# A state-space layer and an outlook layer on one core: a norm chain planned a chunk earlier, a bias that becomes a row of weights, and a product that changes its place in the step

## The chip, the cores and the metric

The kernel runs on one core of one Trainium2 chip. The metric is device time in microseconds (us) of one execution; the kernel before was run three times, and the profile is of one execution more. All data is 32-bit floating point.

The core's engines work from queues of their own, each strictly in the order of its queue, and meet only in semaphores: PE multiplies matrices, ACT applies functions and copies, DVE and POOL do elementwise work, SP issues the transfers. In the code they are `pe`, `ae`, `ve`, `gp` and `sp`. The wrapper `InOrder` (line 40 is its issue, which is why nearly every row of the profile says L40) keeps each engine's instructions in the order in which the program issues them. What an instruction stands behind in its queue is thus read from the program.

## What is computed

There are two layers, each with a residual; the input is 4 images of 384 channels by 4096 positions. The change is in the first.

```python
x = x + L0(group_norm(x))
# L0, per image, positions l in order:
xn = layer_norm(xs) * ln_w + ln_b
xb, z = split(xn @ in_proj_w.T)                 # 768 channels each
xc = silu(causal_conv4(xb) + conv_b)
dt_r, Bm, Cm = split(xc @ x_proj_w.T)           # 24 + 16 + 16
dt = softplus(dt_r @ dt_w.T + dt_b)             # 768 channels
h  = exp(dt * A) * h + (dt * xc) * B            # 768 x 16 states, a recurrence over l
y  = sum_n(h * C) + xc * D
out = (y * silu(z)) @ out_proj_w.T
x = x + L1(group_norm(x))                       # outlook attention, not touched
```

## The kernel before: chunks, units, steps and slots

The first layer (`mamba_layer`) cuts each image's 4096 positions into chunks of 241 (the last of an image has 240), 17 per image, 68 in all. The recurrence of a chunk is cut into 12 **units** (`NU`) of 64 of the 768 channels. One loop runs over **steps** `s`; step `s` runs the recurrence of unit `s`, so a chunk takes 12 steps. In this text a step is named by `m`, its number within the chunk in hand, 0 to 11.

In each step the main loop issues, in this order: the fetch of inputs for unit s+4 (even steps, on SP, eight transfers), the slot EARLY, `s_inputs2` (DVE, half of the product dt*x*B of unit s+1), `s_gate` (DVE, on even steps, for unit s-3), the slot READY, then twice a recurrence `s_scan` on DVE and the decays `s_decay` on ACT (four exponentials of one half of unit s+1), with `s_carry` (ACT) after the first half and `s_save` (DVE, copies the last states away) after the second recurrence. Then come `s_outputs` (POOL, h times C of unit s-1), the slot POOL, `s_inputs` (POOL, the other half of dt*x*B of unit s+2), `s_sum` of unit s-2 (PE; on odd steps ahead of the slot MID, on even steps behind it), MID and LATE.

Everything else, that is, the projections and norms that make a later chunk's inputs (the **front**) and the output projection of a finished chunk (the **end**), is put into these slots by hand. The dictionary `plan` gives, for a step counted from two chunks ahead of the chunk's own start, and for a slot, what is issued; `ends` does so for the end. `parts` looks both up and issues what is due.

The pieces of the front, with the engine of each: `f_load` (SP); the norm chain `f_mean` (PE), `f_center` (DVE, writes `u`), `f_square` (ACT, writes `sq`), `f_var` (PE, `ps_var`), `f_root` (DVE, `vs`), `f_pow` (POOL), `f_rs` (PE, `ps_rs`), `f_scale` (DVE, `u` again); the projections `f_x(0..2)` and `f_z(0..2)` (PE 12 matmul instructions each, copied out by ACT to `xb` and `zs`); `f_conv(0..2)` (PE 16 each, ACT to `xc`); `f_gates` (ACT, Silu of `xc` and `zs` in place, a table load ahead of it and one behind); `f_bc` (PE, `ps_xd`), `f_xd` (ACT copies to `xd`, SP stores it); `f_dt(0..2)` (PE, `ps_dt`), `f_softplus` (ACT, to `dt`; in its wake, in `f_dts`, SP fetches B and C into `bc` in eight transfers and stores `dt` for later fetches), `f_dtx` (DVE, dt*xc, stored by SP for later fetches); `f_b` (PE, replicates B into `bp`). The end is `e_load`, `e_project(0..2)` (PE `ps_out`, ACT copies to `xr`) and `e_store` (DVE statistics, SP).

Buffers that couple the engines: all of the front's and end's PSUM results share a ring of two tiles (`pmm`, tag `mm`); the sums `y` have a single tile, so the first sum of a pair of units waits for `s_gate` of the pair before; the decays have two tiles `da`, one per half; `h` has five; fetched inputs have three.

Where the change bears, the plan before puts, in steps m of the chunk in hand: `f_mean` and `f_center` at the very end of step 2, `f_var` in 5, `f_root` and `f_dt(1)` at the start of 6, then, in the same step 6, the six softplus with `f_dt(2)` among them, `f_rs` at the start of 7, and `f_scale` and `f_dtx` ahead of the recurrences of 7. The projections go from 8 to 1, the gates into LATE of 2, `f_bc` into 4. The end's three projections are in 3, 6 and 8.

Of the kernel before, what the change touches and what calls it, by code (L numbers as in the profile page):

```python
# [5 lines left out]
F32 = mybir.dt.float32  # L6
AF = mybir.ActivationFunctionType
# [3 lines left out]
P = 128  # L11
C = 384
NCB = C // P
DI = 768
NJ = DI // P
NS = 16
RK = 24
KC = 4
TM = 241
CG = 32  # L20
# [64 lines left out]
def mamba_layer(ctx, tc, x, w, x1, sc1, bi1, consts):  # L85
# [78 lines left out]
    def norm_part():  # L164

        if norms:
            try:
                next(norms[0])
            except StopIteration:
                norms.pop(0)  # L170
# [13 lines left out]
    cw = load("cw", [P, NJ, KC])  # L184
    cbias = load("cbias", [P, NJ])
    wx = load("wx", [P, NJ, 2 * NS + RK])
    wdt = wp.tile([2 * NS + RK, DI], F32, tag="wdt", name="wdt")
    sp.dma_start(wdt[2 * NS :, :], w["wdt"])
    dtb = load("dtb", [P, NJ])
    ssum = load("ssum", [P, CG])  # L190
    alog = load("alog", [P, NQ, NG])
    dvec = load("dvec", [P, NJ])
# [10 lines left out]
    sel = wp.tile([2 * NS, NG // 2, P], F32, tag="sel", name="sel")  # L203
    sp.dma_start(sel, w["sel"])
    pw = pmm.tile([P, 2, TM], F32, tag="mm", name="pw")
    for j in range(2 * NJ):
        for cb in range(NCB):
# [4 lines left out]
                start=(cb == 0),  # L212
                stop=(cb == NCB - 1),
# [16 lines left out]
    chunks = [(b, ci, t0, min(TM, L - t0)) for b in range(B) for ci, t0 in enumerate(range(0, L, TM))]  # L230
    NC = -(-L // TM)
    NU = NQ // 2
# [5 lines left out]
    live = {}  # L238
# [15 lines left out]
    def f_center(c):  # L254

        t = c.t
        c.u = front.tile([P, NCB, TM], F32, tag="u", name="u")
        ve.scalar_tensor_tensor(
            c.u[:, :, :t],
            c.xt[:, :, :t],  # L260
            c.sc,
            c.ps[:, 0:1, :t].to_broadcast([P, NCB, t]),
            ALU.mult,
            ALU.subtract,
        )
# [117 lines left out]
    def f_xd(c):  # L383

        t, px = c.t, c.px
        c.xd = front.tile([2 * NS + RK, TM], F32, tag="xd", name="xd")
        ae.copy(c.xd[:, :t], px[: 2 * NS + RK, 0, :t])
        bcd = dram.tile([2, NG, 4, TM], F32, tag="bcd", name="bcd")
        sp.dma_start(bcd[:, :, :, :t].rearrange("k g r t -> (k g r) t"), c.xd[: 2 * NS, :t])
        c.bcd = bcd  # L390

    def f_dt(c, jj):
        t = c.t
        if jj == 0:
            c.dt = front.tile([P, NJ, TM], F32, tag="dt", name="dt")
            c.pdt = {}
        pp = pmm.tile([P, 2, TM], F32, tag="mm", name="ps_dt")
        for h in range(2):
            j = 2 * jj + h
            pe.matmul(  # L400
                pp[:, h, :t], wdt[2 * NS :, j * P : (j + 1) * P], c.xd[2 * NS :, :t], start=True, stop=True
            )
        c.pdt[jj] = pp

    def f_softplus(c, jj):
        t = c.t
        for h in range(2):
            j = 2 * jj + h
            ae.activation(c.dt[:, j, :t], c.pdt[jj][:, h, :t], AF.Softplus, bias=dtb[:, j : j + 1])

    def f_dts(c):
        t = c.t
        f_softplus(c, 0)
        f_dt(c, 2)
        f_softplus(c, 1)
        f_softplus(c, 2)
        c.bc = []
        for k in range(2):
            m = cross.tile([P, NG, TM], F32, tag=f"bc{k}", name=f"bc{k}")
            for r in range(4):  # L420
                sp.dma_start(
                    m[CG * r : CG * (r + 1), :, :t], c.bcd[k, :, r, :t].unsqueeze(0).to_broadcast([CG, NG, t])
                )
            c.bc.append(m)
        c.dtd = dram.tile([NJ, P, TM], F32, tag="dtd", name="dtd")
        sp.dma_start(c.dtd[:, :, :t].rearrange("j p t -> p j t"), c.dt[:, :, :t])

    def f_b(c):

        for g in range(ND):  # L430
            pe.matmul(bp[:, g, : c.t], sel[:, g, :], c.xd[: 2 * NS, : c.t], start=True, stop=True)

    def f_dtx(c):
        t = c.t
# [5 lines left out]

    EARLY, READY, POOL, MID, LATE = range(5)

    def at(f, *args):
        return lambda c: f(c, *args)

    plan = {
        (0, MID): [f_load],
        (2, LATE): [f_mean, f_center],  # L450
        (3, LATE): [f_square],
        (5, MID): [f_var],
        (6, EARLY): [f_root],
        (6, POOL): [f_pow],
        (7, EARLY): [f_rs],
        (7, READY): [f_scale],
        (8, MID): [at(f_x, 0)],
        (9, MID): [at(f_x, 1), at(f_z, 0)],
        (10, LATE): [at(f_x, 2)],
        (11, MID): [at(f_conv, 0), at(f_z, 1)],  # L460
        (12, MID): [at(f_conv, 1)],
        (13, MID): [at(f_conv, 2), at(f_z, 2)],
        (14, LATE): [f_gates],
        (16, MID): [f_bc],
        (16, LATE): [f_xd],
        (17, LATE): [at(f_dt, 0)],
        (18, EARLY): [at(f_dt, 1)],
        (18, READY): [f_dts],
        (19, READY): [f_dtx],
        (22, MID): [f_b],  # L470
    }

# [8 lines left out]
    bp = pbb.tile([P, 2, TM], F32, tag="bp", name="bp")  # L481
# [16 lines left out]
    def unit(n):  # L498
        if not 0 <= n < NU * len(chunks):
            return None  # L500
        if n not in units:
            units[n] = Unit(n)
        return units[n]
# [86 lines left out]
    def s_gate(u):  # L590
        c, t = u.c, u.t
        ve.tensor_mul(c.zs[:, u.j, :t], u.y[:, :t], c.zs[:, u.j, :t])
# [18 lines left out]
    def e_store(c):  # L611
# [12 lines left out]
                )  # L624
            )


    ends = {
        (-3, MID): [e_load],
        (3, MID): [at(e_project, 0)],  # L630
        (6, LATE): [at(e_project, 1)],
        (8, LATE): [at(e_project, 2)],
        (10, READY): [e_store],
    }

    def parts(s, when):

        for k in (s // NU + 3, s // NU + 2, s // NU + 1):
            if 0 <= k < len(chunks):
                for part in plan.get((s - NU * (k - 2), when), []):  # L640
                    if k not in live:
                        c = live[k] = Chunk()
                        c.b, c.ci, c.t0, c.t = chunks[k]
                    part(live[k])
        for k in (s // NU, s // NU - 1):
            if 0 <= k < len(chunks):
                for part in ends.get((s - NU * (k + 1), when), []):
                    part(live[k])

    pending = {}  # L650
    for s in range(-2 * NU, NU * (len(chunks) + 2)):
        k, m = divmod(s, NU)
        if m % 2 == 0 and unit(s + 4) is not None:
            s_fetch(s + 4)
        parts(s, EARLY)
        norm_part()

        if (u := unit(s + 1)) is not None:
            s_inputs2(u)
        if (u := unit(s - 3)) is not None and not u.first:  # L660
            s_gate(u)
        parts(s, READY)

        b, ci = chunks[k][:2] if 0 <= k < len(chunks) else (B, 0)
        if b + 1 < B:
            i, e = divmod(m - 2, 6)
            if ci < NX // 2 and e == 0:
                pending[i] = x_load(b + 1, 2 * ci + i)
            if ci < NX // 2 and e == 2:
                x_stat(b + 1, 2 * ci + i, pending[i])  # L670
            if ci == NX // 2 and m == 6:
                x_coeffs(b + 1)
        for i in range(2):
            if (u := unit(s)) is not None:
                s_scan(u, i)
                if i == 1:
                    s_save(u)
            if (u := unit(s + 1)) is not None:
                s_decay(u, i)
                if i == 0:  # L680
                    s_carry(u)
        if (u := unit(s - 1)) is not None:
            s_outputs(u)
        parts(s, POOL)
        if (u := unit(s + 2)) is not None:
            s_inputs(u)

# [320 lines left out]
def layouts(inputs):  # L1008
# [3 lines left out]
    g = {k: np.asarray(v) for k, v in inputs.items()}  # L1012
    c = np.ascontiguousarray

    def inner(v):
        v = v.reshape(NJ, P, *v.shape[1:])
        return c(np.swapaxes(v, 0, 1))

    a = {}
# [5 lines left out]
    a["cbias"] = inner(g["L0_conv_conv_b"])  # L1025
    wx = g["L0_conv_x_proj_w"]
    a["wx"] = inner(np.concatenate([wx[RK:], wx[:RK]], 0).T)
    a["wdt"] = c(g["L0_conv_dt_w"].T)
    a["dtb"] = inner(g["L0_conv_dt_b"])
    a["alog"] = c(  # L1030
        g["L0_conv_A_log"].reshape(NQ, CG, NG, 4).transpose(3, 1, 0, 2).reshape(P, NQ, NG)
    )
# [16 lines left out]
    r = np.arange(P)  # L1049
    k = np.arange(2 * NS)  # L1050
# [22 lines left out]
```

## Time and profile before

| | |
|---|---|
| three runs | 7261.19, 7263.74 (median), 7266.12 us |
| profiled execution: its own time | 7263.01 us |
| profiled execution: span | 7261.2 us, clock granted to PE 0.895 of full |
| busy share of the span | PE 88%, DVE 78%, POOL 75%, ACT 68% |
| first layer's steady stretch, 120 to 5860 us | PE 5033.63, DVE 4892.31, POOL 4833.87, ACT 4251.41 us busy of 5740; clock 0.88 |
| second layer, 5985 to 7261 us | PE 1226.91 us busy of 1276; clock 0.98 |
| one period of the steady stretch | `dtx` at 2591.16 and again at 2676.49 us: 85.33 us for a chunk of 12 steps |

A page of the profile lists, for each group of instructions, its busy time, the mean of one, and the idle time of the engine ahead of it with what ended it. The timeline gives instructions of one engine in order of time: start, duration of the run of them, names, count, and in brackets the idle time before and what ended it. A wait "<-PE ps_rs" was ended by PE's writing of `ps_rs`. The chain of work is followed back from the last instruction, at each step to what released it. Idle time of an engine that nobody waits for costs nothing.

### The profile page before, as it was taken

Reading aid. Unit: us, or ns where it says so; the run is one execution under the profiler, and the core shown is the slowest. Engines: PE = TensorE matmul, PEld = TensorE weight load, DVE = VectorE, ACT = ScalarE, POOL = GpSimd, SP = SyncE. Lnnn points to the kernel's source line nnn. Section 1 sums busy time; section 2 is a strip of 40 time slices with the busy share of each in tenths; the row PEclk is TensorE's granted clock in tenths of the full one; section 3 lists DMA queues with packets and bytes.
Section 4 is the critical chain, followed back from the end, with each engine's and each line's share of the span. In section 5 each row is a group of like instructions: output and inputs, shape, how many; then the busy total and the mean of one; then the engine's idle time right before and its main releaser. Section 6 shows DMA issues by size and latency. Waiting matters only on the chain.

```text
span 7261.2 us, 112696 instructions
## 1 busy us (share of the span) xinstructions
PE 6411.3 (88%) x40440; PEld 4301.2 (59%) x40440; DVE 5628.1 (78%) x5688; ACT 4933.4 (68%) x10865; POOL 5426.0 (75%) x2101
## 2 busy tenths in 40 slices
PE   6888888888888888888888888888888868999999
PEld 5666566565565666655656666655656634555555
DVE  4888888888888888888888888888888874444444
ACT  3777777777777777777777777777777754544454
POOL 4888888887887888888888888888888872433443
PEclk9888888888888888888888888888888878999999
DMA  4544444444454444445444444444444434554444
GB/s 127 130 121 119 111 110 108 115 114 115 126 127 110 113 110 110 108 115 128 120 122 108 112 113 111 109 106 118 112 116 116 111 98 147 169 169 168 164 164 151
DMA packets 899707, 893.21 MB, mean 123 GB/s; under 512 B 121856, under 2 KB 858930, under 8 KB 898634
## 3 DMA queue, kind: packets, MB, share of 16 engines
q1 hardware_dynamic: 899146, 886.00, 45.8%
q8 instruction: 319, 5.23, 0.3%
q14 instruction: 242, 1.98, 0.1%
HBM read 659.99 MB, written 225.68 MB: 122 GB/s over the span
## 4 chain that ended last, share of the span: by engine, by line
PE 62%; DVE 26%; ACT 7%; issue 3%; DMA 1%; POOL 1%; SPq 0%; DVEq 0%; POOLq 0%; ACTq 0%
DVE h L40 20%; PE y L40 17%; PE ps_in L40 11%; PE ps_cv L40 9%; PE ps_out L40 6%; PE psv L40 5%; PE pso L40 4%; ACT da L40 3%; PE ps L40 3%; PE psa L40 2%; PE ps_dt L40 2%; DVE dtx L40 2%; ACT L40 1%; PE ps_ln L40 1%; DVE at L40 1%
## 5 line engine op out<-in xcount | busy, mean ns | idle before, releaser
L40 POOL TENSOR_TENSOR h<-h,bc 128x1928 f32<-128x1928 f32 (+1 forms) x816 | 3232.2, 3961 | 795.8 <-DVE st L40 457.1
L40 DVE TENSOR_TENSOR_SCAN h<-da,h 128x968 f32<-128x968 f32 (+1 forms) x1632 | 3450.8, 2155 | 159.9 <-ACT h L40 157.6
L40 ACT ACTIVATE da<-dtr,aneg 128x241 f32<-128x241 f32 (+1 forms) x6528 | 3036.0, 465 | 734.7 <-DVE h L40 528.0
L40 POOL TENSOR_TENSOR h<-dxr,bc 128x964 f32<-128x964 f32 (+1 forms) x816 | 1688.6, 2069 | 93.0 <-PE y L40 67.5
L40 PE MATMUL y<-h,ssum 128*32 128x241 f32 (+1 forms) x13056 | 1638.4, 411 | 19.2 <-POOL h L40 19.2
L40 PEld LDWEIGHTS y<-h,ssum 128*32 128x32 f32 x13056 | 732.0, 120 | 802.4 <-issue 395.8
L40 PE MATMUL ps_in<-u,win 128*128 128x241 f32 (+1 forms) x4896 | 1086.2, 373 | 4.5 <-DVE u L40 2.4
L40 PEld LDWEIGHTS ps_in<-u,win 128*128 128x128 f32 x4896 | 919.5, 191 | 149.9 <-ACT da L40 48.0
L40 POOL TENSOR_TENSOR bd<-ain,own 99x1188 f32<-99x1188 f32 x192 | 413.0, 2180 | 794.3 <-DMA ain<-ad 660.6
L40 DVE TENSOR_TENSOR h<-dxr,bp 128x964 f32<-128x964 f32 (+1 forms) x816 | 940.2, 1152 | 39.6 <-POOL h L40 16.8
L40 PE MATMUL ps_cv<-xb,cdiag 128*128 128x241 f32 (+1 forms) x3264 | 714.0, 371 | 11.0 <-DVE sc L40 9.8
L40 PE MATMUL ps_dt<-xd,wdt 24*128 24x241 f32 (+1 forms) x816 | 394.7, 635 | 349.8 <-ACT dt L40 137.2
L40 PEld LDWEIGHTS ps_cv<-xb,cdiag 128*128 128x128 f32 x3264 | 608.5, 190 | 106.2 <-ACT da L40 49.2
L40 PE MATMUL y<-xc,ddiag 128*128 128x241 f32 (+1 forms) x816 | 329.7, 493 | 321.3 <-DVE zs L40 321.3
L40 PE MATMUL psv<-wv,xp 128*128 128x384 f32 x1728 | 588.7, 492 | 0.8 <-ACT vst L40 0.8
L40 ACT ACTIVATE bd<-ain,own 99x324 f32<-99x324 f32 x704 | 334.7, 556 | 295.6 <-PE ps L40 282.7
L40 PE MATMUL ps_out<-zs,wout 128*128 128x241 f32 (+1 forms) x2448 | 533.3, 366 | 0.0
L40 PEld LDWEIGHTS ps_dt<-xd,wdt 24*128 24x128 f32 x816 | 231.9, 312 | 473.3 <-ACT dt L40 182.0
L40 PEld LDWEIGHTS ps_out<-zs,wout 128*128 128x128 f32 x2448 | 473.4, 193 | 39.3
L40 DVE TENSOR_TENSOR fold<-fold,ps 128x192 f32<-128x192 f32 (+1 forms) x768 | 211.1, 303 | 339.0 <-PE ps L40 325.7
L40 PEld LDWEIGHTS psv<-wv,xp 128*128 128x128 f32 x1728 | 320.9, 190 | 224.9 <-issue 8.5
L40 DVE SCALAR_TENSOR_TENSOR u<-u,bc,ps_rs 128x723 f32<-128x723 f32 (+1 forms) x68 | 65.8, 968 | 469.4 <-PE ps_rs L40 469.4
(96 smaller groups left out, 5427.8 us busy)
## 6 DMA issues: line engine op xcount, KB each, us to landing
dxr<-dxd SPq DMA_DIRECT2D x1536, 120.5 KB
dtr<-dtd SPq DMA_DIRECT2D x1536, 120.5 KB
bc<-bcd SPq DMA_DIRECT2D x512, 120.5 KB
vin<-vd SPq DMA_DIRECT2D x384, 148.5 KB
vd<-vst SPq DMA_DIRECT2D x96, 576.0 KB
dtd<-dt SPq DMA_DIRECT2D x64, 723.0 KB
dxd<-dtx SPq DMA_DIRECT2D x64, 723.0 KB
xs<-in_x SPq DMA_DIRECT2D x64, 384.0 KB
```

The lines of the kernel that those rows point to most:

```text
L40: return self.tc.keep_in_program_order(issue(*args, **kwargs))
```

## The change

Four things are altered, all in the first layer.

1. The plan. The norm chain of a chunk is issued twelve to thirteen steps earlier than before, against the steps that use it, and its pieces are spread: load in step 0, mean in 1, centre ahead of the recurrences of 2, variance in 5, root in 6, `f_rs` in 7, and `f_scale` after the recurrences of 7. `u` gets a second buffer. The projections move up to steps 7 to 0, the gates to LATE of step 0, `f_bc` and `f_xd` to 2, `f_dt` to 3 and 4. The end's projections go to 2, 4 and 5, its store to 8.
2. `xd` is one tile for the whole layer with an added row of ones, and `wdt` gets the bias as a 25th row, so that the matmul adds dt's bias.
3. `f_dt` copies its result from PSUM to `dt` at once (one copy for each two of the six blocks), and softplus runs in place over all 1446 columns in LATE of step 5.
4. `f_dtx` is issued in a new slot SCAN in step 6, after the second recurrence and before `s_save`.

```diff
+    KX = 2 * NS + RK + 1
+    xd = wp.tile([2 * CG, TM], F32, tag="xd", name="xd")
+    gp.memset(xd, 1.0)
+    wdt = wp.tile([KX, DI], F32, tag="wdt", name="wdt")
...
-        c.u = front.tile([P, NCB, TM], F32, tag="u", name="u")
+        c.u = front.tile([P, NCB, TM], F32, tag="u", name="u", bufs=2)
...
     def f_dt(c, jj):
...
-                pp[:, h, :t], wdt[2 * NS :, j * P : (j + 1) * P], c.xd[2 * NS :, :t], start=True, stop=True
+                pp[:, h, :t], wdt[2 * NS :, j * P : (j + 1) * P], xd[2 * NS : KX, :t], start=True, stop=True
             )
-        c.pdt[jj] = pp
-
-    def f_softplus(c, jj):
-        t = c.t
-        for h in range(2):
-            j = 2 * jj + h
-            ae.activation(c.dt[:, j, :t], c.pdt[jj][:, h, :t], AF.Softplus, bias=dtb[:, j : j + 1])
-
-    def f_dts(c):
-        t = c.t
-        f_softplus(c, 0)
-        f_dt(c, 2)
-        f_softplus(c, 1)
-        f_softplus(c, 2)
+        ae.copy(c.dt[:, 2 * jj : 2 * jj + 2, :t], pp[:, :, :t])
+
+    def f_softplus(c):
+        t = c.t
+        ae.activation(c.dt[:, :, :t], c.dt[:, :, :t], AF.Softplus)
         c.bc = []
...
     plan = {
-        (0, MID): [f_load],
-        (2, LATE): [f_mean, f_center],
-        (3, LATE): [f_square],
-        (5, MID): [f_var],
-        (6, EARLY): [f_root],
-        (6, POOL): [f_pow],
-        (7, EARLY): [f_rs],
-        (7, READY): [f_scale],
-        (8, MID): [at(f_x, 0)],
-        (9, MID): [at(f_x, 1), at(f_z, 0)],
-        (10, LATE): [at(f_x, 2)],
-        (11, MID): [at(f_conv, 0), at(f_z, 1)],
-        (12, MID): [at(f_conv, 1)],
-        (13, MID): [at(f_conv, 2), at(f_z, 2)],
-        (14, LATE): [f_gates],
-        (16, MID): [f_bc],
-        (16, LATE): [f_xd],
-        (17, LATE): [at(f_dt, 0)],
-        (18, EARLY): [at(f_dt, 1)],
-        (18, READY): [f_dts],
-        (19, READY): [f_dtx],
+        (-12, MID): [f_load],
+        (-11, MID): [f_mean],
+        (-10, READY): [f_center],
+        (-10, LATE): [f_square],
+        (-7, LATE): [f_var],
+        (-6, EARLY): [f_root],
+        (-6, POOL): [f_pow],
+        (-5, MID): [f_rs],
+        (-5, LATE): [f_scale],
+        (7, MID): [at(f_x, 0)],
+        (8, LATE): [at(f_x, 1), at(f_z, 0)],
+        (9, LATE): [at(f_x, 2), at(f_z, 1)],
+        (10, LATE): [at(f_conv, 0)],
+        (11, LATE): [at(f_conv, 1), at(f_z, 2)],
+        (12, LATE): [at(f_conv, 2), f_gates],
+        (14, MID): [f_bc],
+        (14, LATE): [f_xd],
+        (15, LATE): [at(f_dt, 0), at(f_dt, 1)],
+        (16, LATE): [at(f_dt, 2)],
+        (17, LATE): [f_softplus],
+        (18, SCAN): [f_dtx],
         (22, MID): [f_b],
     }
...
     ends = {
         (-3, MID): [e_load],
-        (3, MID): [at(e_project, 0)],
-        (6, LATE): [at(e_project, 1)],
-        (8, LATE): [at(e_project, 2)],
-        (10, READY): [e_store],
+        (2, LATE): [lambda c: e_project(c, 0)],
+        (4, LATE): [lambda c: e_project(c, 1)],
+        (5, LATE): [lambda c: e_project(c, 2)],
+        (8, READY): [lambda c: e_store(c)],
     }
...
                 s_scan(u, i)
-                if i == 1:
+            if i == 1:
+                parts(s, SCAN)
+                if u is not None:
                     s_save(u)
...
-    a["wdt"] = c(g["L0_conv_dt_w"].T)
-    a["dtb"] = inner(g["L0_conv_dt_b"])
+    a["wdt"] = c(np.concatenate([g["L0_conv_dt_w"].T, g["L0_conv_dt_b"][None]], 0))
```

Within one slot `parts` issues the latest chunk's pieces first, then the earlier ones', and an ending chunk's last. The loop over steps begins 12 steps earlier, for the earlier norm chains of the first chunks.

More of the change, by code (lines that the diff above doesn't have):

```diff
@@ L186, in mamba_layer @@
     wx = load("wx", [P, NJ, 2 * NS + RK])
-    wdt = wp.tile([2 * NS + RK, DI], F32, tag="wdt", name="wdt")
+    KX = 2 * NS + RK + 1
+    xd = wp.tile([2 * CG, TM], F32, tag="xd", name="xd")
+    gp.memset(xd, 1.0)
+    wdt = wp.tile([KX, DI], F32, tag="wdt", name="wdt")
     sp.dma_start(wdt[2 * NS :, :], w["wdt"])
-    dtb = load("dtb", [P, NJ])
     ssum = load("ssum", [P, CG])
@@ L385, in f_xd @@
         t, px = c.t, c.px
-        c.xd = front.tile([2 * NS + RK, TM], F32, tag="xd", name="xd")
-        ae.copy(c.xd[:, :t], px[: 2 * NS + RK, 0, :t])
+        ae.copy(xd[: 2 * NS + RK, :t], px[: 2 * NS + RK, 0, :t])
         bcd = dram.tile([2, NG, 4, TM], F32, tag="bcd", name="bcd")
-        sp.dma_start(bcd[:, :, :, :t].rearrange("k g r t -> (k g r) t"), c.xd[: 2 * NS, :t])
+        sp.dma_start(bcd[:, :, :, :t].rearrange("k g r t -> (k g r) t"), xd[: 2 * NS, :t])
         c.bcd = bcd
@@ L395, in f_dt @@
             c.dt = front.tile([P, NJ, TM], F32, tag="dt", name="dt")
-            c.pdt = {}
         pp = pmm.tile([P, 2, TM], F32, tag="mm", name="ps_dt")
@@ L430, in f_b @@
         for g in range(ND):
-            pe.matmul(bp[:, g, : c.t], sel[:, g, :], c.xd[: 2 * NS, : c.t], start=True, stop=True)
+            pe.matmul(bp[:, g, : c.t], sel[:, g, :], xd[: 2 * NS, : c.t], start=True, stop=True)
     def f_dtx(c):
@@ L438, in f_dtx @@
         sp.dma_start(c.dxd[:, :, :t].rearrange("j p t -> p j t"), dtx[:, :, :t])
-    EARLY, READY, POOL, MID, LATE = range(5)
+    EARLY, READY, SCAN, POOL, MID, LATE = range(6)
     def at(f, *args):
@@ L448, in mamba_layer, with parts @@
     plan = {
-        (0, MID): [f_load],
-        (2, LATE): [f_mean, f_center],
-        (3, LATE): [f_square],
-        (5, MID): [f_var],
-        (6, EARLY): [f_root],
-        (6, POOL): [f_pow],
-        (7, EARLY): [f_rs],
-        (7, READY): [f_scale],
-        (8, MID): [at(f_x, 0)],
-        (9, MID): [at(f_x, 1), at(f_z, 0)],
-        (10, LATE): [at(f_x, 2)],
-        (11, MID): [at(f_conv, 0), at(f_z, 1)],
-        (12, MID): [at(f_conv, 1)],
-        (13, MID): [at(f_conv, 2), at(f_z, 2)],
-        (14, LATE): [f_gates],
-        (16, MID): [f_bc],
-        (16, LATE): [f_xd],
-        (17, LATE): [at(f_dt, 0)],
-        (18, EARLY): [at(f_dt, 1)],
-        (18, READY): [f_dts],
-        (19, READY): [f_dtx],
+        (-12, MID): [f_load],
[19 more added lines that the diff above has]
+        (18, SCAN): [f_dtx],
         (22, MID): [f_b],
     }
+    ends = {
+        (-3, MID): [lambda c: e_load(c)],
+        (2, LATE): [lambda c: e_project(c, 0)],
+        (4, LATE): [lambda c: e_project(c, 1)],
+        (5, LATE): [lambda c: e_project(c, 2)],
+        (8, READY): [lambda c: e_store(c)],
+    }
+    def parts(s, when):
+        for k in range(s // NU + 3, s // NU - 2, -1):
+            if 0 <= k < len(chunks):
+                r = s - NU * (k - 2)
+                due = plan.get((r, when), []) + ends.get((r - 3 * NU, when), [])
+                if due and k not in live:
+                    c = live[k] = Chunk()
+                    c.b, c.ci, c.t0, c.t = chunks[k]
+                for part in due:
+                    part(live[k])
     das = [pda.tile([P, 1024], F32, tag=f"da{i}", name=f"da{i}") for i in range(2)]
@@ L625, in e_store @@
             )
-    ends = {
-        (-3, MID): [e_load],
-        (3, MID): [at(e_project, 0)],
-        (6, LATE): [at(e_project, 1)],
-        (8, LATE): [at(e_project, 2)],
-        (10, READY): [e_store],
[L634 to L648, printed above, removed]
     pending = {}
-    for s in range(-2 * NU, NU * (len(chunks) + 2)):
+    for s in range(-3 * NU, NU * (len(chunks) + 2)):
         k, m = divmod(s, NU)
```

## The prediction

> **What bounds the kernel now.** I read the page's busy shares first: PE 88%, DVE 78%, POOL 75%, ACT 68%. No engine is full, and the second layer (1276 us) isn't touched, so the question is what paces one chunk of the first, 85.33 us from one `dtx` to the next. The waits come next.
>
> ```profile
> DVE u L40 <- PE ps_rs L40: 469.4, 68, 7.6
> POOL h L40 <- DVE st L40: 457.1, 220, 8.0
> DVE u L40 <- PE ps_ln L40: 202.4, 65, 28.8
> ```
>
> The columns are total, times, longest. Once a chunk `f_scale` waits 6.9 us for `f_rs`, and POOL, which needs the recurrences queued behind it, waits as long. The timelines of DVE and PE around it show why.
>
> ```profile
> 3010.75 1.16 DVE L40 TENSOR_TENSOR h<-dxr,bp 128x960 f32<-128x960 f32 x1 [1.37 <-DMA bc<-bcd]
> 3016.87 0.97 DVE L40 SCALAR_TENSOR_TENSOR u<-u,bc,ps_rs 128x723 f32<-128x723 f32 x1 [4.96 <-PE ps_rs L40]
> 3017.75 1.66 DVE L40 TENSOR_TENSOR dtx<-dt,xc 128x1446 f32<-128x1446 f32 x1
> ```
>
> ```profile
> 3006.78 1.97 PE L40 MATMUL ps_dt<-xd,wdt 24*128 24x241 f32 x4 [2.02 <-ACT dt L40]
> 3008.68 1.17 PE L40 MATMUL y<-xc,ddiag 128*128 128x240 f32 x2
> 3009.78 3.42 PE L40 MATMUL y<-h,ssum 128*32 128x240 f32 x16
> ...
> 3013.78 2.61 PE L40 MATMUL ps_out<-zs,wout 128*128 128x241 f32 x12
> 3016.23 0.60 PE L40 MATMUL ps_rs<-ident,vs 121*128 121x121 f32 x4
> ```
>
> `f_rs` stands on PE behind `f_dt(2)`, which waits for softplus, a sum and an output projection. The stall costs PE too: it idles until the next gate and comes back at half speed. Of what follows, the chain of work (start, us, what) shows where PE's backlog meets ACT:
>
> ```profile
> 2978.10 2.46 PE ps_in L40 x12
> 2980.56 0.02 issue
> 2980.58 0.81 ACT zs L40 x2
> ...
> 2985.23 1.28 ACT L40
> 2986.51 0.01 issue
> 2986.53 1.41 ACT xc L40
> 2987.94 1.30 ACT zs L40
> 2989.23 0.02 issue
> 2989.25 1.28 ACT L40
> ```
>
> PE is in this chain without a gap from 2939.87 to 2980.56: it is the pace from step 8 to step 1. Then ACT is, with the two gates between two table loads (5.3 us), until decays let DVE go on. In steps 3 to 7 DVE and the stall set the pace. So I cost three legs: PE, ACT, DVE.
>
> **What the Trainium skill says.** "TensorE: Matmul & The Clock Gate", Part 1 (What's actually happening): PE drops to half clock after an idle window of about 3.4 us and needs as long of work to come back. The trace agrees: after 3.96 us of idle, the 18 instructions of a sum took 4.53 us, against 2.36 warm. "ScalarE: Activation LUTs", What ACT_TABLE_LOAD costs: a load is about 1283 ns and a drain of 1380 comes with it. The load agrees (349.0 us for 272); the drain does not, since silu starts 0.02 us after the load, so I use 1.30. "ScalarE activation tables: per-element evaluation and per-set limits", What a function is on this engine: the cost is the same whichever table is read. The trace agrees (softplus 462 ns, Identity 455 to 460), so softplus over 1446 columns is priced like Silu of 1446, 1.41 us.
>
> **The change, part by part.** m is the step in the chunk, T(m) the start of its first recurrence.
>
> *Softplus and bias.* Six activations from PSUM at 462 ns (about 2.3 us in a run) become three copies of 482 columns (559 ns by the row of `xb`) and one pass of 1.41: 3.1 us. Both loads stay. That is 0.8 us more on ACT, in steps 3 to 5, where it has room. What goes is PE's wait inside `f_dt`, since each result is copied at once. 25 rows instead of 24 I cost at nothing: time goes with the 241 columns (0.22 us a warm instruction in every row of 128, 32 or 24 rows).
>
> *SP.* In step 5 the eight fetches of `bc` and the store of `dt` come ahead of step 6's eight fetches for unit 10, and the store waits for softplus. These fetches (1.8 us per four) then end about 31 us after T(2); POOL wants them at 40. The store of `dtx` follows, 1 us after `dtx`, the fetch of unit 12 behind it as before. `f_load` is issued two steps ahead of `f_mean`, 12 us. Nothing; without this cover a late fetch would stop POOL for as long as it is late.
>
> *The stall.* `f_rs` now comes on PE right behind a sum in step 7, `f_scale` after the recurrences. By the sums below `f_rs` is done some 5 us ahead. The 6.9 us go. What is late next is found by walking round the loop.
>
> *Leg 1, PE, from the gate of step 8 to `f_conv(2)`.* The gate frees `y`; PE has idled about 5 us (its work of step 7 ends early), so it starts cold, as now. In queue order, by the timeline's and the chain's pieces: sum 4.53, `f_x(1)`+`f_z(0)` 5.09 and 0.5 for the end of the slow stretch, sum 1.76, `f_x(2)`+`f_z(1)` 5.09, `f_b` 1.00, sum 2.36, `f_conv(0)` 3.45, sum 1.76, `f_conv(1)`+`f_z(2)` 5.90, sum 2.36, `f_conv(2)` 3.25. That is 37.05 us. (Before it was 40.7 to the end of `f_z(2)`: the output projection, 3.5, has left this stretch.) Nothing in it waits: each needs a copy by ACT that is 4 us or more old.
>
> *Leg 2, ACT, to T(2).* Now `f_gates` stands directly behind the copy of `f_conv(2)`, in LATE of step 0, and the decays of unit 2 stand behind `f_gates`. Copy 0.87, load, silu, silu, load 5.30, four decays and the carry 2.13: 8.3 us. DVE alone would be at step 2 some 5 us earlier, so this is a new wait of about that size, on `h` by ACT. The wait for `ps_ln` (3 us) goes inside it.
>
> *Leg 3, DVE, from T(2) to the gate of step 8.* A step is 5.41 us (two recurrences 4.27, save 0.08, `s_inputs2` 1.07), 5.74 with a gate. T(5) = T(2)+16.56. In step 6 `f_root` is first in DVE's queue and waits for `f_var`. PE: the sum of step 4 starts when `f_dt(1)` is done, 11.3; half cold 3.5, `f_dt(2)` 0.9, `e_project(1)` 3.1, sum 1.76, `f_var` 1.42: 22.0. DVE is there at 20.9, so it waits 1.15. The trace doesn't show this arrangement: warm, it would be 0, all cold 2.5. T(6) = 22.05+0.12+1.07+0.33 = 23.6. Step 6: recurrences 4.25, `dtx` 1.57, save 0.1, `s_inputs2` 1.07: T(7) = 30.6. `dtx` in front of the save holds up the second decay and POOL by 1.57; the decay ends 1 us before it is wanted. Softplus ends at 26.8, ahead of `dtx` (27.8). Step 7: 4.35, `f_scale` 0.88, `s_inputs2` 1.07, gate 0.40: 37.3.
>
> *The sum.* 37.05 + 8.3 + 37.3 = 82.65 us a chunk, against 85.3: 2.65 less. POOL needs 12 x 6.03 + 1.07 = 73.4, so it isn't the bound. Of 68 chunks 66 have a full period: 175 us. At the start two more norm chains come ahead of the first recurrence, one of them with nothing beside it: 8 us (57.42 to 65.31 for the first; 0 to 16). The profiled execution took 7263.01, 0.7 less than the median: 7263 - 175 + 8 = 7096, say 7097.
>
> *Bounds.* `f_root` 0 or 2.5 us, and 0.5 either way for sums in leg 1 (two sums back to back took 3.02, not 4.12): 81.05 to 84.5 us a chunk, 6985 to 7220.
>
> **The rivals.**
>
> *A, nothing takes the stall's place.* If ACT's free third swallowed the gates, DVE's own 71.3 (66.9 for twelve steps, 4.4 for norm, `dtx` and statistics) and POOL's 73.4 would set some 75 us a chunk: 7263 - 66 x 10.3 + 8 = 6590. For it: the busy shares. Against: in the chain ACT's gates already stand on the path, and now come one step sooner after PE.
>
> *B, `f_root` takes over from `f_scale`.* It is first in its step too, behind two output projections. If it waits 3.8 us instead of 1.15, the gain is gone: 7271, within 0.2% (about what a measurement of this kernel tells from no change). For it: PE at half clock would add 5 us to what stands ahead of `f_var`. Against: PE has some 11 us of work without a gap by then.
>
> *C, slower: the train stays cold.* If PE does `f_x(1)`, `f_z(0)` at half clock, leg 1 grows by 5.1 us and the chunk is 82.65 + 5.1 = 87.75: 7263 + 66 x 2.4 + 8 = 7430. It decides from 2.65 us on, some 12 instructions more at half clock. For it: around `ps_dt` PE now stays slow for 13.8 us. Against: waits of 1 to 2 us lie in that stretch, none in this one.
>
> **How the numbers follow.** The forecast has 0.74, A 0.06, B 0.08, C 0.12. So faster by over 0.2% is 0.80, within 0.2% 0.08, slower 0.12. The range takes in the forecast's own, 6985 to 7220, and B: 6985 to 7275.
>
> **What would show it.** DVE's wait for `ps_rs` gone and that for `ps_ln` small; `h` on DVE waiting for ACT about 5 us at one step a chunk, with silu and loads just ahead of it in the chain; `vs` waiting about 1 us for `ps_var`; `dtx` to `dtx` 82 to 84 us; still 272 table loads. I am wrong if DVE doesn't wait for ACT behind the gates, if another wait of over 2 us a chunk appears, or if PE runs `f_z(0)` at half clock.

## The result and the profile after

| | before | after |
|---|---|---|
| median of six runs (lowest to highest), us | 7263.41 (7261.19 to 7266.12) | 7236.03 (7233.96 to 7237.27) |
| profiled execution, us | 7263.01 | 7234.33 |
| granted clock | 0.895 | 0.912 |
| VectorE (DVE) busy, us | 5628.1 | 5651.4 |
| sum of all waits of DVE, us | 1574.9 | 1524.4 |

The ratio is 0.9962, with a 95% interval of 0.9949 to 0.9975: 27 us less, where 167 were forecast. The books close on DVE: 50 us less waiting, 23 more busy. But that small balance is made of large items. First the waits of all engines, then those of DVE alone (total, times, longest).

```profile
POOL h L40 <- DVE st L40: 661.0, 385, 10.5
...
DVE h L40 <- ACT h L40: 480.5, 266, 5.5
...
DVE vs L40 <- PE ps_var L40: 219.3, 67, 10.7
```

```profile
DVE u L40 <- PE ps_ln L40: 28.3, 5, 26.6
DVE zs L40 <- PE y L40: 21.7, 67, 6.1
DVE u L40 <- PE ps_rs L40: 4.0, 2, 2.1
```

The stall of `f_scale` (`ps_rs`, 469.4) is gone, and so is most of `ps_ln` (202.4): 639 us. In their place `h` waits for ACT (157.6 before, 323 more) and `vs` for `ps_var` (9.1 before, 210 more). POOL waits 204 us more for the recurrences (457.1 before). But its wait of 294.6 us, which the profile puts down to the store of `dtx`, is gone but for 0.7, and the sum of all its waits is 1785 us against 1815. For the transfers the prediction had neither a loss nor a gain.

Now one chunk of the kernel after, whose T(2) is at 3572.85 and whose next T(2) comes at 3658.19, 85.34 us later. DVE (start, us, what):

```profile
3572.85 4.24 DVE L40 TENSOR_TENSOR_SCAN h<-da,h 128x968 f32<-128x968 f32 x2 [4.19 <-ACT h L40]
...
3594.72 0.17 DVE L40 TENSOR_TENSOR st<-h,da 128x8 f32<-128x8 f32 x1
3598.28 0.22 DVE L40 TENSOR_SCALAR vs<-ps_var 121x1 f32<-121x1 f32 x2 [3.39 <-PE ps_var L40]
...
3603.95 1.64 DVE L40 TENSOR_TENSOR dtx<-dt,xc 128x1446 f32<-128x1446 f32 x1
...
3611.00 0.96 DVE L40 SCALAR_TENSOR_TENSOR u<-u,bc,ps_rs 128x723 f32<-128x723 f32 x1
```

`u` is scaled and `dtx` made without a wait. `f_root` (`vs`) waits 3.39 us, and the recurrence of step 2 waits 4.19 for ACT. PE ahead of `f_root`:

```profile
3580.40 1.89 PE L40 MATMUL ps_dt<-xd,wdt 25*128 25x241 f32 x8 [2.47 <-ACT xd L40]
3584.18 1.17 PE L40 MATMUL y<-xc,ddiag 128*128 128x241 f32 x2 [1.89 <-DVE zs L40]
3585.28 3.43 PE L40 MATMUL y<-h,ssum 128*32 128x241 f32 x16
3588.64 1.97 PE L40 MATMUL ps_dt<-xd,wdt 25*128 25x241 f32 x4
3590.54 1.17 PE L40 MATMUL ps_out<-xr,ident 128*128 128x241 f32 x2
3591.50 3.63 PE L40 MATMUL ps_out<-zs,wout 128*128 128x241 f32 x12
3595.06 1.83 PE L40 MATMUL y<-h,ssum 128*32 128x241 f32 x16
3596.82 1.43 PE L40 MATMUL ps_var<-onesc,sq 128*121 128x1 f32 x12
```

The sixteen instructions of a sum take 3.43 us at 3585.28 and 1.83 at 3595.06: the first is at half clock. How long that lasts is seen in stretches of 3.41 us (their columns: length, then busy time of PE, PEld, DVE, ACT, POOL, then PE's granted clock, DMA share, GB/s):

```profile
3579.97:3583.38 3.41, 1.89 (x8) 1.40 (x8) 3.38 (x4) 3.10 (x10) 3.41 (x2) 0.99 0.46 118
3583.38:3586.80 3.42, 2.62 (x10) 1.25 (x12) 3.42 (x6) 2.23 (x5) 3.42 (x2) 0.50 1.09 218
3586.80:3590.21 3.41, 3.41 (x14) 1.72 (x10) 3.38 (x4) 2.69 (x7) 3.12 (x3) 0.50 0.99 209
3590.21:3593.62 3.41, 3.41 (x9) 2.62 (x9) 3.41 (x3) 1.66 (x4) 3.41 (x2) 0.51 0.22 48
3593.62:3597.04 3.42, 3.42 (x26) 2.13 (x25) 1.24 (x2) 1.78 (x5) 3.42 (x2) 1.00 0.01 2
...
3610.69:3614.10 3.41, 0.61 (x2) 0.50 (x2) 3.38 (x8) 2.69 (x8) 3.41 (x2) 0.50 0.50 146
3614.10:3617.52 3.42, 3.42 (x18) 1.29 (x16) 3.42 (x3) 1.07 (x3) 3.42 (x2) 0.51 0.67 173
3617.52:3620.93 3.41, 3.41 (x20) 2.99 (x17) 3.36 (x4) 3.10 (x8) 2.30 (x2) 1.00 0.98 243
```

With bounds laid on a grid of 3.413 us, every stretch is wholly fast or wholly slow. The clock changes at points of that grid alone, here three steps after the drop, then two. The rest of the trace agrees: the first layer has 147 slow stretches, each of one, two, three or four whole steps. "TensorE: Matmul & The Clock Gate", Part 1 (What's actually happening), in the Trainium skill says that the window of 3413 ns runs freely, without regard to the program; the trace agrees. I had cited that section for the length of the window and not drawn the consequence.

Last, the chain of work around the gates:

```profile
3646.36 3.47 PE ps_cv L40 x16
3649.83 0.02 issue
3649.85 0.81 ACT xc L40 x2
...
3651.98 1.41 ACT xc L40
3653.39 1.30 ACT zs L40
3654.71 1.28 ACT L40
...
3658.19 4.25 DVE h L40 x2
```

It is leg 2 as forecast: convolution, copy, load, two Silu, load, decays, recurrence.

### The profile page after: what moved, and what is told of

Same layout as the page of the kernel before. It is cut to its first block, busy times and chain, and to the rows that moved or that the text cites. A ratio compares the mean times of both kernels' runs of the same rounds, so it can differ in the third digit from the quotient of the medians.

```text
span 7232.5 us, 112296 instructions
## 1 busy us (share of the span) xinstructions
PE 6332.4 (88%) x40440; PEld 4261.8 (59%) x40440; DVE 5651.4 (78%) x5688; ACT 4972.4 (69%) x10729; POOL 5426.5 (75%) x2102
## 4 chain that ended last, share of the span: by engine, by line
PE 54%; DVE 24%; ACT 13%; issue 4%; DMA 2%; POOL 2%; SPq 0%; DVEq 0%; ACTq 0%; POOLq 0%
DVE h L40 19%; PE y L40 14%; PE ps_in L40 11%; PE ps_cv L40 8%; ACT da L40 6%; PE psv L40 5%; PE ps_out L40 4%; PE pso L40 4%; PE ps L40 3%; PE psa L40 2%; POOL h L40 2%; ACT L40 2%; ACT xc L40 2%; ACT zs L40 1%; PE ps_dt L40 1%
## 5 line engine op out<-in xcount | busy, mean ns | idle before, releaser
L40 PE MATMUL ps_out<-zs,wout 128*128 128x241 f32 (+1 forms) x2448 | 585.7, 392 | 0.0
L40 PEld LDWEIGHTS y<-xc,ddiag 128*128 128x128 f32 x816 | 159.5, 229 | 665.2 <-issue 466.9
L40 PEld LDWEIGHTS ps_out<-zs,wout 128*128 128x128 f32 x2448 | 508.9, 208 | 51.7
L40 PE MATMUL ps_dt<-xd,wdt 25*128 25x241 f32 (+1 forms) x816 | 270.8, 478 | 166.8 <-ACT xd L40 166.8
L40 ACT ACTIVATE zs<-ps_in,bxz 128x241 f32<-128x241 f32 (+1 forms) x408 | 166.0, 459 | 329.5 <-PE ps_in L40 329.5
```

Source lines behind the costliest of these rows:

```text
L40: return self.tc.keep_in_program_order(issue(*args, **kwargs))
```

## The experiments

Two theories were set against each other at first. **Lock (L)**: a slow stretch of PE ends at a point of the clock's grid, so what a shorter path saves comes back as a longer slow stretch, and the chunk stays at 25 grid steps, 85.33 us. Both kernels sit there: the kernel before shows 85.33 or 85.34, the kernel after 85.33 to 85.35 in its long rows of equal chunks, and 83.2 and 87.4 in turn elsewhere, which is the same in the mean. **Sum (S)**: the new waits simply have their sizes, and each microsecond added to the path or taken from it shows one for one; for the first two runs with idle matmuls S also said that the clock is of no account. Later runs ask which part of the change pays and which costs. Each experiment was run once, where nothing else is said, beside the kernel before on the same chip (7262.31 to 7264.66 us); executions of one kernel that were repeated lie within 7 us of each other.

**A delay on DVE.** dt*x of two (or four) of its six blocks is multiplied a second time, some 0.56 (or 1.12) us a chunk; in the first two runs on the kernel after, in the third on the kernel before.

```diff
         ve.tensor_mul(dtx[:, :, :t], c.dt[:, :, :t], c.xc[:, :, :t])
+        ve.tensor_mul(dtx[:, :2, :t], c.dt[:, :2, :t], c.xc[:, :2, :t])
```

> The changed kernel with a third of the product dt*x done twice on DVE, about 0.56 us more at each chunk, on DVE's leg. Theory L (lock): PE's clock changes only on a grid of 3.413 us, a slow stretch ends on a grid point, and so the chunk's period is held at 25 grid steps, 85.33 us; a small delay shortens a slow stretch by as much, and the period stays 85.33: 7236 us within 10. Theory S (plain sum): the new waits add up to what the old one was, so 0.56 us more cost 66 times as much: about 7273 us.

> The changed kernel with two thirds of dt*x done twice, about 1.1 us more on DVE at each chunk, twice what the first delay cost. In the last image's undisturbed chunks the first delay left the mean period at 85.33. Theory L: it stays at 25 grid steps on the mean over these chunks, or goes up by whole steps in some of them (84 to 88 alternating); the total isn't 66 times the delay. Theory S: 73 us more than the changed kernel, 7309 us, with the period of every undisturbed chunk 86.4 to 86.5.

> The kernel before with a third of dt*x done twice, 0.56 us more on DVE at each chunk. Theory L: its period, too, is held at 85.33 by the grid, so its undisturbed chunks stay at 85.33 and the total within 15 us of 7263. Theory S: 37 us more, 7300.

Measured: 7266.48, 7266.40 and 7268.83 us, which is 30, 30 and 6.5 us more. DVE's busy time grew by 79, 122 and 40 us, in the first two by more than the planned 37 and 74. So the second delay cost nothing beyond the first, and S is refuted in all three. Chunks in the long rows stay at 85.33 in all three. But L's simple form missed the first total: 30 us more, not 10. About 6 us of this in each image are in the ten chunks behind each image's first, where the kernel after isn't in step with the grid.

**PE kept at full clock in the kernel after.** Idle matmuls, written where the real result follows: 5 in `e_project(0)`, 4 ahead of `f_dt(1)`, 12 ahead of `f_x(0)`; then the first two places alone, then the third alone; then all three again, in four executions.

```diff
+    def fill(pp, n):
+        for _ in range(n):
+            pe.matmul(pp[:, 0, :], ident, win[:, 0, :TM], start=True, stop=True)
...
+        if cb == 0:
+            fill(po[:, 1:2, :], 5)
...
+        if jj == 1:
+            fill(pp, 4)
...
+        if jj == 0:
+            fill(pp, 12)
```

> The changed kernel with idle matmuls (weights times identity, written ahead of the real result into the same tile) in the three gaps of PE: 5 in the first output projection of the end, 4 ahead of the second matmul of dt, 12 ahead of the first projection; 2 us, 1.7 us and 5 us of PE at full clock. Theory L: PE never falls to half clock, the wait for ps_var falls from 3.3 to under 1 us, leg 1 from 36.3 to about 34.5, the period is no multiple of 3.413 and lies at 80 to 81.5 us: 6920 to 7000 us. Theory S (POOL's pace and new waits, clock of no account): the idle matmuls gain nothing, 7236 us or some 10 more.

> The changed kernel with idle matmuls only around dt (5 and 4), steps 2 to 3. Theory L: the slow stretch of steps 3 to 5 is gone, and the wait for ps_var with it; one slow stretch is left, ahead of step 8, so the period can still settle on the grid: 24 steps are 81.92 us, about 7010 us, or it runs free at 82 to 83. Theory S: 7236 us as before.

> The changed kernel with idle matmuls only ahead of the first projection (12), step 7. The slow stretch at step 8 is gone and leg 1 is 1.8 us shorter. Theory L: the stretch of steps 3 to 5 is left, and it can take up the 1.8 us, so that the period stays at 85.33 and the time at 7236 within 15, or falls by a whole grid step to 81.92. Theory S: leg 1's 1.8 us are gained, 66 times: about 7117 us.

> The kernel after with the idle matmuls of the second experiment (5 ahead of e_project(0)'s result, 4 ahead of f_dt(1), 12 ahead of f_x(0)), timed in rounds. The lock theory and the sum theory both expect the 6934 us of the single look again, within 15 us; ratio to before 0.953 to 0.957.

Measured: 6934.35, 7040.76 and 7123.16 us; in the four executions 6931.96 (6931.54 to 6933.17), ratio to before 0.9543, interval 0.9527 to 0.9559. This beats both kernels and is the best version found. The clock is 0.984, the chunk 79.25 us (80.16 with the statistics of an image), and no common phase with the grid is left. DVE's waits in the second run, whose idle matmuls stand only ahead of `f_root`:

```profile
DVE h L40 <- ACT h L40: 487.0, 271, 5.5
...
DVE vs L40 <- PE ps_var L40: 20.0, 4, 11.4
```

`ps_var` fell from 219.3 to 20.0, 199 us, the time fell by 195, and the chunk from 25 to 24 grid steps: 81.92 in its longest row, 80.9 rising towards it elsewhere. So the slow stretch in steps 3 to 5 is what `f_root` waits for. S as put on record expected no gain in these two runs and is refuted; as a plain sum of a removed wait it gives the second run's time as well as L does. In the third run the plain sum was right and L was not: S expected about 7117 us and 7123.16 were measured, and the chunks take 81 to 88 us in no fixed period, where L expected 85.33 or a whole step less. So the lock is common and no law.

**The same for the kernel before**, to see what the change is worth with the clock out of play: idle matmuls in `f_var`, ahead of `f_dt(0)`, `f_dt(1)` and `f_x(0)` (4, 0, 4, 8; then 4, 5, 4, 10; then 4, 5, 6, 12).

```diff
         pv = pmm.tile([P, 2, TM], F32, tag="mm", name="ps_var")
+        fill(pv, 4)
...
         pp = pmm.tile([P, 2, TM], F32, tag="mm", name="ps_dt")
+        if jj == 1:
+            fill(pp, 4)
```

> The kernel before with idle matmuls in PE's gaps: 4 ahead of the variance's, 4 ahead of the second of dt's, 8 ahead of the first projection's. If the clock is what held both kernels at one period, this one falls to about 81 to 82.5 us a chunk, 6970 to 7080 us, still above the changed kernel with idle matmuls (6934) by 40 to 150 us: what the change is worth without the clock, forecast at 2.65 us a chunk. Theory S: the old wait for f_rs is a wait on softplus's and the sum's order, not on the clock; 7200 or more.

> The kernel before with idle matmuls also ahead of the first of dt's (5), and 10 ahead of the first projection, so that the gap of 2.15 us that was left ahead of dt's second is closed and PE is at full clock throughout. In the run before, the chunks without a slow stretch took 80.1 us. Theory L with what that run showed: every chunk at 80.1, no grid, 6930 to 6960 us, and so the same as the changed kernel with idle matmuls (6934) within 30: with the clock out of play the change moves DVE's waits from f_rs and ps_ln to the gates, and its gain is 0 to 1 us a chunk, not 2.65. If the forecast's 2.65 us hold with a warm PE: 80.16 + 2.65 a chunk, 7110 us.

> The kernel before with idle matmuls in four places (4 in f_var, 5 ahead of f_dt(0), 6 ahead of f_dt(1), 12 ahead of f_x(0)). If the clock and its grid are what the two plans share (lock theory), no slow stretch is left, the granted clock is above 0.98, chunks take 79.5 to 80.2 us with no common period, and the time is 6930 to 6990: then the change is worth 0 to 60 us on a warm engine. If the change's stall of f_scale costs its full 2.65 us a chunk on a warm engine (the prediction's sum), the time is 6934 + 175 = 7110 with no slow stretch in the records.

Measured: 7132.81, 7055.41 and 7063.73 us, clock 0.943, 0.974 and 0.975. All three missed: slow stretches were left, whatever was added. Warm chunks of the second run take 79.8 us against 79.25. This suggests about half a microsecond of worth a chunk, but the difference of whole runs (7055 or 7064 to 6932) says more; as no kernel before ran warm throughout, it stays open.

**The gates one step later in the warm kernel after.**

```diff
-        (12, LATE): [at(f_conv, 2), f_gates],
+        (12, LATE): [at(f_conv, 2)],
+        (13, LATE): [f_gates],
```

> The changed kernel with all idle matmuls and the two gates put one step later, in LATE of step 1. What is left with a warm PE is DVE's wait behind the gates, 4.2 us at step 2 and 2 us at step 1. With the decays of unit 2 ahead of the gates, the wait moves to step 3 and is 1 to 3 us: 77.5 to 79 us a chunk, 6800 to 6870 us. If instead what follows the gates on PE (B, C and dt's low-rank part) is then late for softplus, 6930 or more.

Measured: 7248.2 us. PE now waits for the gates:

```profile
PE ps_xd L40 <- ACT xc L40: 295.0, 68, 7.4
```

`f_bc` had stayed in step 2 and needs them; PE idles 4.3 us a chunk, `f_dt` comes late and a slow stretch is back, the second of the two cases expected. Gates can't move without what reads them.

**Parts of the change alone.** On the kernel before: the norm chain with its new places and the second `u`; the bias row, copies and softplus in one pass (`f_dt` in LATE of 5 and EARLY of 6, softplus in READY of 6); both, with mean, centre and square about a step later than in the change; and that last one with idle matmuls. The softplus part was run warm too.

```diff
-        (18, EARLY): [at(f_dt, 1)],
-        (18, READY): [f_dts],
+        (18, EARLY): [at(f_dt, 1), at(f_dt, 2)],
+        (18, READY): [f_softplus],
```

```diff
-        (0, MID): [f_load],
-        (2, LATE): [f_mean, f_center],
-        (3, LATE): [f_square],
...
+        (-12, MID): [f_load],
+        (-10, LATE): [f_mean],
+        (-9, READY): [f_center],
+        (-9, LATE): [f_square],
```

> The kernel before with the norm chain alone put a chunk earlier, at the slots of the changed plan, and a second buffer for u; projections, gates, dt, end as before. Theory L and the moved wait: the 6.9 us behind f_rs and the 3 behind ps_ln go, and the gates stay where ACT has room for them, so nothing takes their place but some 2 us behind softplus: 6 to 8 us less of path; on the grid 24 or 23 steps, 81.92 or 78.51 us, 6810 to 7040 us. Rival: the norm chain's stall hides another of its size in the same step (softplus, its loads and dt*x), so that it gains under 2 us: 7130 us or more.

> The kernel before with dt's bias in the weights, copies out of PSUM at once and softplus in one pass alone; dt's second and third matmul follow at the start of step 6, softplus ahead of step 6's recurrences on ACT, all else as before. PE no longer waits for softplus inside dt, f_rs comes 2 to 4 us sooner. Theory L: the period falls only if a whole grid step or a fraction of it in a cycle of chunks is reached: 85.33 (7263) or about 83 to 84 (7110 to 7180). Theory S: 2 to 4 us a chunk, 7000 to 7130.

> The softplus part and the norm chain ahead together, with the projections, convolutions, gates, f_bc, dt and the ends left in their old places (the mean, the centring and the square sit one or half a step later than in the change, so that the centring doesn't wait for f_z(2)'s reading of the second buffer of u). If it is the moved projections, convolutions, gates and ends that give back the gain, this is at least as fast as softplus alone (7147): 6980 to 7110 with f_scale's wait gone, on a grid of 24 steps (81.92 us) or below. If it is the norm chain's new place that gives it back, chunks return to 25 steps: 7230 to 7280.

> The softplus part alone (bias row, copies, one pass; everything else in the old places) with idle matmuls (4 in f_var, 4 ahead of f_dt(0), 2 ahead of f_dt(1), 10 ahead of f_x(0)). If the moved steps of the whole change cost something even on a warm engine, this is below the warm kernel after: 6850 to 6930. If the warm kernels are bound by VectorE's work alone, 6934 within 30. If a slow stretch is left (granted clock under 0.97), 7000 to 7080.

> The kernel of norm chain and softplus together with idle matmuls (10 ahead of f_x(0), 10 ahead of f_dt(0), 4 ahead of f_dt(1)), timed in rounds. In its profile TensorE is at half clock for some 14 to 17 us of each 81.6 us chunk. If that is what bounds it, as it did the kernel after (304 us from the same remedy), 6710 to 6850 and granted clock above 0.97. If VectorE's and GpSimd's own work is the bound by now (dt*x takes 5 us beside GpSimd's product), 6950 to 7014.

Norm chain alone: 7271.09 us, no gain. That lies in the rival's range, but for a reason that the rival did not name: the stall moved to `f_center`. In the place that the change gives it, this writes the buffer of `u` that `f_z(2)`, still in its old place, has yet to read:

```profile
DVE u L40 <- PE ps_in L40: 384.5, 66, 28.0
```

Softplus alone: 7146.97 us, 118 less, with a period of 24.5 grid steps in the mean (83.2 and 84.0 in turn). DVE's wait for `ps_rs` is 352.0 us instead of 469.4, 117 less: PE reaches `f_rs` sooner. **Both: 7014.07 us, 249 less than before and 222 less than the whole change.** DVE's waits in it:

```profile
DVE h L40 <- ACT h L40: 168.4, 120, 3.4
DVE u L40 <- PE ps_ln L40: 120.6, 65, 26.8
DVE dtx L40 <- ACT dt L40: 58.6, 62, 8.3
...
DVE vs L40 <- PE ps_var L40: 12.9, 3, 5.5
```

Neither of the change's two new waits is there. Softplus with idle matmuls gave 6977.4 us, between the values expected; norm and softplus with idle matmuls 7196.16, ratio 0.9908 (0.9891 to 0.9924), which is *slower* than without them, and I had expected 6710 to 6850. In its trace `dtx` waits for softplus:

```profile
DVE dtx L40 <- ACT dt L40: 299.5, 67, 12.4
```

ACT waits 347.5 us for `ps_dt` where it waited 112.6. PE's timeline shows what the ten idle matmuls ahead of `f_dt(0)` do (each is two entries):

```profile
5190.15 7.39 PE L40 MATMUL ps_dt<-win,ident 128*128 128x241 f32 x20 [2.68 <-ACT xd L40]
5197.47 1.08 PE L40 MATMUL ps_dt<-xd,wdt 25*128 25x241 f32 x4
```

They don't fill the gap. They begin when `xd` is there, with 2.68 us of idle still ahead of them, run in part at half clock, and so put 7.39 us in front of `f_dt(0)`, on the path to `dt`. No run with fewer of them in this kernel was made.

**The moved steps alone**, each added to the kernel of norm and softplus: the middle (projections to dt*x in the change's places), and the ends.

```diff
-        (14, LATE): [f_gates],
+        (12, LATE): [at(f_conv, 2), f_gates],
...
-        (19, READY): [f_dtx],
+        (18, SCAN): [f_dtx],
```

```diff
-        (3, MID): [lambda c: e_project(c, 0)],
+        (2, LATE): [lambda c: e_project(c, 0)],
```

> The kernel of norm chain and softplus together (7014 us), with the middle of the plan at the change's early places (f_x, f_z, f_conv, f_gates, f_bc, f_xd, f_dt, f_softplus, and dt*x behind the recurrence), the ends left in their old places. If the gates at step 2 are what gives the gain back (VectorE waits 4.2 us for ScalarE's h behind them, 2 at the step before), VectorE's wait for h from ScalarE returns to 400 to 480 us in all and the time is 7160 to 7260. If the early ends give it back, that wait stays and the time is 7014 or less, down to 6800 since dt*x no longer takes 5 us.

> The kernel of norm chain and softplus together (7014 us), with only the ends at the change's early places (output projections at steps 2, 4 and 5, store at 8). If the gates' place gives the gain back, 7014 within 70, and VectorE's wait for h from ScalarE stays under 250 us. If the ends give it back, 7160 to 7260.

Measured: 7304.6 and 7057.31 us. The middle alone costs 290 us, more than the 222 that the change gives back in all, and more than expected (7160 to 7260). The ends cost 43, as expected within 70; `dtx` waits 248.3 us for ACT there, where it waited 58.6. DVE's waits with the middle early:

```profile
DVE h L40 <- ACT h L40: 541.5, 227, 5.5
DVE zs L40 <- PE y L40: 186.0, 116, 6.3
```

The first grew by 373 us, the second by 179. A likely part of it is the early gates. This is ACT in the kernel that left them late:

```profile
4021.08 0.81 ACT L40 ACTIVATE xc<-ps_cv,cbias 128x241 f32<-128x241 f32 x2 [0.40 <-PE ps_cv L40]
...
4028.19 1.28 ACT L40 ACT_TABLE_LOAD   x1
```

There the gates' load comes 7.1 us after the copy of `f_conv(2)` begins. In between ACT copies `f_z(2)` and finishes the eight decays of the next unit, and DVE waits 1.89 us behind the gates. In the changed plan the load follows the copy at once (3649.85, 3650.68 on ACT), with PE's longest train just ahead, and DVE waits 4.2. Moving the gates alone was not run.

## Why the prediction was wrong, step by step

| step | forecast, us a chunk | measured in the chunk above |
|---|---|---|
| leg 1, gate of step 8 to `f_conv(2)` | 37.05 | 36.34 (3613.49 to 3649.83) |
| leg 2, to T(2) | 8.3 | 8.36 (3649.83 to 3658.19) |
| leg 3, T(2) to the gate of step 8 | 37.3 | 40.5 (3572.85 to 3613.34) |
| sum | 82.65 | 85.2 |

**The step that failed is leg 3's wait of `f_root`**: "it waits 1.15. The trace doesn't show this arrangement: warm, it would be 0, all cold 2.5". It waited 3.39 us in this chunk, 3.27 in the mean (219.3 us, 67 times), but from 0.4 to 5.7 in the single chunks of the steady stretch. That PE began the sum when forecast (11.33 us after T(2) against 11.3) was luck: `f_dt(1)` was done at 9.4, and the sum then waited 1.89 us for the gate. Then the sum took 4.46 us, not "half cold 3.5"; `f_dt(2)` 1.9, not 0.9; `e_project(1)` 4.5, not 3.1: 3.4 us in all, because PE was still at half clock where I had it warm again. `f_var` ended at 25.4, not 22.0. (DVE was there at 22.0, not 20.9: this chunk has 1.07 us of statistics ahead of it. In the equal chunks of the last image, which have none, it waits 4.29 and the chunk takes 85.33 all the same: the end of `f_var` sets the pace.) My bound for "all cold" was itself added up too low. I had let a slow stretch end after so much work of PE; it ends at a grid point, here the third. Idle matmuls there gave 195 us back, to 7041, where my sum had 7097.

So rival B is what happened, in place and mechanism: `f_root` takes over, with 3.4 us where I had put 3.8 as the point of no gain. Its own number, 7271, was 35 us too high. "PE has some 11 us of work without a gap by then", my reason against it, is where I went wrong: of that work the first 9.4 us (3584.18 to 3593.6) ran slow. The clock had dropped at 3583.38, in the idle gap of 1.89 us ahead of the sum and after one of 2.47 ahead of `f_dt`, and it was back three windows later, not after half a sum.

**What was right.** The stall's end, leg 1 and its cold start, and leg 2: the new wait for `h` is 4.2 us at step 2. There are smaller ones of 2.05 at step 1 and 0.7 at step 0 that I had not listed; they lie inside leg 1 and don't lengthen it. Softplus in one pass costs 1411 ns, a copy 556. 272 table loads take 349.0 us, as before. Rival C (PE cold through `f_z(0)`) didn't come. At the start the first recurrence comes at 139.10 us against 125.44, 14 later, for a forecast of 8 (0 to 16).

**What the sum couldn't see.** It priced the plan as given, and the plan's gain and loss cancel: norm chain and softplus are worth 249 us, the early middle costs 290 on top of them, and the whole comes to 27. The parts don't add: the ends cost 43 on the kernel with a late middle, yet the whole change is 69 faster than the kernel with an early middle and late ends (in which the norm chain's first pieces also come a step later). The wait on `h` that I booked as the price of the change was the price of a move that its other parts don't need: left at home, that wait stays at 168 us, against 158 before.

**What stays open.** Which of the middle's moves carries the 290 us wasn't run singly; the trace points at the gates and at `y`. That slow stretches end on the grid is shown; that this holds the chunk at 25 steps is shown for the delays in the long rows of chunks and fits 24 steps (81.92) in two other kernels, but norm with softplus runs mostly at 81.6 us, off the grid, the idle matmuls ahead of `f_x(0)` alone gained what a plain sum said, and nothing here says beforehand which kernel will lock.

## What to carry to other kernels

Where an engine has a clock that follows its load, price the stretch after each idle gap at the slow rate up to a point of the clock's grid (here the second or third after the drop), and ask for each wait on that engine whether it lies inside. Before believing the sum of a plan with many moves, price each group of moves alone: here two carried the whole gain and a third ate it. And, as far as the trace suggests it, put a long piece on ACT where other work separates it from its input, not directly behind the train that feeds it.

## What the runs showed that I had not expected

- The clock's grid as a pacemaker: a delay of 0.56 us a chunk cost 6.5 us in 66 chunks; steady periods of 85.33, 83.6 and 81.92 us are 25, 24.5 and 24 steps of 3.413.
- A stretch doesn't need to be empty for the clock to drop: the two windows ahead of the drop at 3583.38 had PE busy 1.38 and 1.89 us of 3.41. This is not the idle window of 3.4 us that the prediction reckoned with; here the measurement decides. And one fully busy window didn't always bring it back (3586.80 to 3590.21).
- In the kernel of norm and softplus `dtx` takes 5.06 us in the median instead of 1.64. POOL's and DVE's timelines there:

```profile
4053.11 3.93 POOL L40 TENSOR_TENSOR h<-h,bc 128x1928 f32<-128x1928 f32 x1
4056.99 3.58 POOL L40 TENSOR_TENSOR h<-dxr,bc 128x964 f32<-128x964 f32 x1
```

```profile
4053.51 5.05 DVE L40 TENSOR_TENSOR dtx<-dt,xc 128x1446 f32<-128x1446 f32 x1 [0.48 <-ACT dt L40]
```

`dtx` starts 0.4 us behind POOL's product and ends 1.5 us after it; POOL's next product then takes 3.58 us where the median is 2.07. "SBUF — State Buffer", section "SBUF: two separate sides", in the Trainium skill says that a DVE operation with two inputs in SBUF and a POOL operation that reads SBUF exclude each other for their whole length. The trace agrees: counted from the end of POOL's first product (4057.04), `dtx` takes 1.5 us, close to its 1.64, and counted from the end of `dtx` (4058.56) POOL's next takes 2.0. DVE is busy 216 us more than in the kernel before, all of it in `dtx`. A better place for `dtx` in that kernel might gain some of this; it was not tried.
